# A decoder of mixed layers on one core: routed experts in two groups of blocks instead of one

## The chip, the cores and the metric

The kernel runs on one core of a Trainium2 chip. The metric is the device time of one execution in microseconds; the median over runs counts. Its engines are PE (matrix products; its weight loads are listed as PEld), DVE (vector), ACT (activations), POOL (the general engine, which also issues the scatters), and SP, which issues the plain DMAs. Each works through its own queue in order, and they wait for each other by semaphores.

## What is computed

Twelve layers follow each other on 2048 tokens of width 128 (32 sequences of 64), each with a residual and a layer norm: `x = layernorm(x + layer(x))`. Three of them matter here. Before the change's place comes a cross attention with 16 heads of width 8 (`l1x`), then a layer of experts (`l1f`), then a causal self attention of the same heads (`l2a`). The expert layer sends each token through one of eight two-layer networks, the one whose logit is largest:

```python
logits = xf @ Wr.T + br
expert_idx = jnp.argmax(logits, axis=-1)
h = jax.nn.relu(jnp.einsum('td,efd->etf', xf, W1) + b1[:, None, :])   # 128 -> 512
y = jnp.einsum('etf,edf->etd', h, W2) + b2[:, None, :]                 # 512 -> 128
out = y[expert_idx, jnp.arange(xf.shape[0])]
```

## The kernel before

Tokens lie in four blocks of 512 (`NBLK`), each of four tiles of 128 tokens. Work is written as steps: `sp.at(step, place, f)` puts a piece of work at a step and a place in it, and `Steps.run` (L269) calls the pieces in that order. PE's instructions keep exactly this order. DVE's and ACT's keep it only in the stretches in `sp.fixed` (from four steps before the end of the experts on); elsewhere a scheduler orders them, and it orders POOL's and SP's everywhere.

The attention (`attn8`, L675) goes through 16 units, four to a block: scores with mask (`s`), maximum and difference on DVE (`mx`, `p`), the exponential on ACT, transposes (`ptps`, copied by ACT to `pT`), values (`o`), normalising on DVE (`rec`, `a`), a transpose (`aT`) and the output product (`y`), then sum and layer norm. The layer norm's `rstd` (L436) is two operations on POOL. The last block is handled in halves.

The expert layer is `sorted_experts` (L1441). While the attention runs, `routed` (L1381) does, for pieces of tiles: logits (`rps`, L343), the comparison and the first best expert on DVE, a running count per expert (`before`, `tally` L1332), ranks by two products (`inc`, `rank` L1345), the row of each token (`slot`), and one indirect DMA per token tile from POOL (L1364) that scatters the tokens' rows, each with its token number, into a DRAM buffer `sorted_x`, in which every expert has room for all 2048 tokens.

When all tokens are counted, `tables` (L1460) takes one product for the totals (`cnt`) and some fifteen small DVE operations to a table: for each of `NTL = 16 + 7 = 23` tiles of 128 sorted rows, its expert and its first row. The engines then read the table's numbers into registers (`values_load`, L1497) and use them as addresses: SP for the load of each tile's rows (`xsorted`, L1379), ACT for a copy of the expert's first weights, 512 columns (L1508), DVE for a copy of its second weights and biases, 644 columns (L1510), both out of the big buffer `wbig` where all eight experts lie. A tile (`tile_`, L1546) is then a transpose (`xsT`, L1514) of the tile two ahead, the first product (`hps`, four matmuls), a relu with bias in four parts (`hs`, two on ACT at L1530 and two on DVE at L1528, in turn), and for the tile before it the second product (`yps`), the sum with the bias on DVE (`ysorted`, L1541) and a scatter of the rows into `token_y` by token number (L1364), issued by POOL. All 23 tiles stand at one step after the attention.

On the way back, `rows_back` loads a block's rows from `token_y` after all scatters (`z`), DVE adds the residual, the layer norm follows, `turn_x` transposes (`xTps`, copied to `xT`), and the next attention's keys, queries and values (`proj`, `k`, `kx`, `q`, `vps`) of block 0 start. Block 0's norm is done by DVE and ACT in halves; the others' come at later steps. Between the last tile and block 0's transposes stand the keys and values of three blocks of a later cross attention (`early`, L705), which only need the context; their results lie in `wbig` over weights no longer needed.

Of the kernel before, what the change touches and what calls it, by code (L numbers as in the profile page):

```python
# [30 lines left out]
NTL = NTT + NEXP - 1  # L31
XR = D + 4
SORTED = NEXP * NT + NEXP * P - P
# [10 lines left out]
def _constants():  # L44
# [12 lines left out]
    c["base1"] = np.broadcast_to((e * f(NT) - f(1)) / f(P), (P, 8))  # L57
    c["base2"] = np.broadcast_to((e * f(CAP) - f(1)) / f(P), (P, 8))
    c["less1"] = np.broadcast_to(e * f(NT) - f(P), (P, 8))
# [222 lines left out]
class Decoder:  # L282
# [66 lines left out]
    def setup(self):  # L349
# [42 lines left out]
        self.sorted_x = self.tc.dram_tile([SORTED, XR], F32, name="sorted_x")  # L392
        self.chosen_x = self.tc.dram_tile([NEXP * CAP, XR], F32, name="chosen_x")
        self.token_y = [self.tc.dram_tile([NT, D], F32, name=f"token_y{i}") for i in range(2)]
# [15 lines left out]
    def clear(self, sp, first):  # L410

        self.cleared = []
        zero = {}

        def start():
            z = zero[0] = self.q2([P, 3, XR], "zero")
            self.nc.gpsimd.memset(z, 0.0)
            self.nc.gpsimd.memset(z.bitcast(I32)[:, :, D:], 1 << 16)

        def part(dst, o, n, m, d):  # L420
            v = dst[o : o + P * n * m, :].rearrange("(p n m) d -> p n m d", n=n, m=m)
            i = self.nc.sync.dma_start(v, bc(zero[0][:, 0:m, 0:d], 1, n))
            self.cleared.append(i.ins)

        sp.at(first, 7, start)
        parts = [(self.sorted_x, i * P * 15, 5, 3, XR) for i in range(9)]
        parts += [(self.chosen_x, 0, 5, 1, XR), (self.token_y[1], 0, 16, 1, D)]
        for i, p in enumerate(parts):
            sp.at(first + 1 + 2 * i, 7, lambda p=p: part(*p))
# [245 lines left out]
    def attn8(self, sp, base, name, src=None, rope=None, scale=1.0, row=None, mask=(None, None), has_out=True, split=False, number=False, turned=None, ahead=None, held=False):  # L675
# [136 lines left out]
        sp.at(base - 4, 2.4 if held else 3, start)  # L812
# [5 lines left out]
        for blk in range(NBLK):  # L818
            for i in range(3):
                n = base + 4 * blk - 4  # L820
                at = (n + 1 + (i + 1) // 2, 4 + i % 2 / 2) if held and blk else (n + i, 4)
                sp.at(*at, lambda blk=blk, i=i: prepare(blk, i))
            sp.at(base + 4 * blk + (1 if split and not has_out else 2), 5.5, lambda blk=blk: resid(blk))
            if halved(blk):
                sp.at(*((base + 16, 6.5) if turned is None else (base + 16, 5.8)), lambda blk=blk: turn(blk, (0, 2)))
                sp.at(*((base + 17, 6.5) if turned is None else (base + 17, 2.1)), lambda blk=blk: turn(blk, (2, 2)))
                sp.at(*((base + 16, 6.4) if turned is None else (base + 16, 5.3)), lambda: normal_rest(0))
                sp.at(*((base + 17, 6.4) if turned is None else (base + 17, 2)), lambda: normal_rest(1))
            else:
                at = (base + 4 * blk + 8, 6)  # L830
                if split and blk == NBLK - 2:
                    at = (base + 16, 2.1 if has_out else 4.1)
                sp.at(*at, lambda blk=blk: turn(blk, (0, TPB)))
# [498 lines left out]
    def tally(self, st, t0, n, base):  # L1332

        before = st["before", t0] = self.sb([P, TPB + 1, 8], "before", 3)
        last = st.get("sum", base)
        self.nc.gpsimd.tensor_copy(before[:, 0, :], last)
        for t in range(n):  # L1340
            self.tt(before[:, t + 1, :], last, st["oh"][:, t0 + t, :], ALU.add)
            last = before[:, t + 1, :]
        st["sum"] = last
# [37 lines left out]
    def routed(self, sp, st, ready, wr, br, base, rows, dst, bound, gated):  # L1381


        def logits(t0, i):
# [18 lines left out]
        def chosen(t0, n):  # L1403
            self.first_of(st.pop(("lg", t0))[:, 0:n, :], st["oh"][:, t0 : t0 + n, :])
            self.tally(st, t0, n, self.c[base])
# [5 lines left out]
        def scatter(t0, t):  # L1411
            blk, i = divmod(t0 + t, TPB)
            self.scatter(
                dst, self.xfull[blk][:, i, :], st["at", t0][:, t : t + 1], st["done"], self.cleared, bound
# [10 lines left out]
        ]  # L1425
        for t0, m, logit, compared, first, second, ranked, scattered in pieces:
# [14 lines left out]
    def sorted_experts(self, sp, name, ready, fetched, tiles, back):  # L1441
# [5 lines left out]
        k = dict(done=[], y=[])  # L1447
# [12 lines left out]
        def tables():  # L1460

            ps = self.ps8("G", "cnt")
            self.mm(ps[:, 0:8], self.ones, k["sum"])
# [14 lines left out]
            table = k["table"] = self.once([P, 2, NTL], "tiles", I32)  # L1478
            jump = self.once([P, 8], "jump")
            nc.vector.tensor_scalar(jump, size, -1.0, float(NT), ALU.mult, ALU.add)  # L1480
# [8 lines left out]
            for j in range(NTL):  # L1489
                if j % 3 == 0:  # L1490
                    xg[j // 3] = self.q2([P, 3, XR], "xsorted")
                row = number(1, j, SORTED - P, mybir.EngineType.SP)
                self.load_after(xg[j // 3][:, j % 3, :], self.sorted_x[bass.ds(row, P), :], k["done"])
            for j in range(AHEAD):
                weights(j)

        def number(i, j, most, engine):  # L1497
            return nc.values_load(
                k["table"][0:1, i, j : j + 1], engines=[engine], min_val=0, max_val=most,
# [3 lines left out]
        def weights(j):  # L1503
            if j < NTL:
                w1, w2 = wts[j] = self.q2([P, 4 * P], "w1"), self.q4([P, EROW - 4 * P], "w2")
                most = (NEXP - 1) * EROW
                at = number(0, j, most, mybir.EngineType.Activation)
                nc.scalar.copy(w1, self.big[:, bass.ds(at, 4 * P)])  # L1508
                at = number(0, j, most, mybir.EngineType.DVE) + 4 * P
                nc.vector.tensor_copy(w2, self.big[:, bass.ds(at, EROW - 4 * P)])  # L1510

        def turn(j):
            ps = self.ps8("G", "xsT")
            nc.tensor.transpose(ps[:, 0:P], xg[j // 3][:, j % 3, 0:D], self.ident)  # L1514
            xT = self.sb([P, P], "xsT", 3)
            nc.scalar.copy(xT, ps[:, 0:P])
            st[j] = xT

        def hidden(j):
            ps = self.ps8("G", "hps").rearrange("p (c n) -> p c n", n=P)  # L1520
            w1, w2 = wts[j]
            for c in range(4):
                self.mm(ps[:, c, :], w1[:, c * P : (c + 1) * P], st[j])
            h = self.q2([P, 4, P], "hs")
            for c in range(4):
                b1 = w2[:, 4 * P + c : 4 * P + c + 1]
# [4 lines left out]
            st[j] = h  # L1531

        def second(j):
            h, (_, w2) = st.pop(j), wts.pop(j)
            ps = self.ps8("G", "yps")
            for c in range(4):
                self.mm(ps[:, 0:D], h[:, c, :], w2[:, c * P : (c + 1) * P], c == 0, c == 3)
            if j % 4 == 0:
                ys[j // 4] = self.q2([P, 4, D], "ysorted")
            y = ys[j // 4][:, j % 4, :]  # L1540
            self.summed = nc.vector.tensor_tensor(out=y, in0=ps[:, 0:D], in1=w2[:, 4 * P + 4 :], op=ALU.add).ins  # L1541
            at = xg[j // 3].bitcast(U32)[:, j % 3, D : D + 1]
            self.scatter(self.token_y[0], y, at, k["y"], [], NT - 1)
            weights(j + AHEAD)

        def tile_(j):  # L1546
            if j == 0:
                turn(0)
                turn(1)
            if j + 2 < NTL:  # L1550
                turn(j + 2)
            hidden(j)
            if j:
                second(j - 1)
            if j == NTL - 1:
                second(j)

        def rows_back(b):
            z[b] = self.q2([P, TPB, D], "z")
            self.load_after(z[b], self.token_rows(0, b), k["y"] + [[], [self.turned_at], [self.wide], [self.wide]][b])  # L1560

        def added(b):
            self.tt(z[b], z[b], self.xt[b], ALU.add)
            if b:
                k["moments", b] = self.moments(b, z[b])
            else:
                self.norm(b, z.pop(b), "both")
# [11 lines left out]
        sp.at(ready + 10, 0, tables)  # L1579
        for j, at in enumerate(tiles):  # L1580
            sp.at(*at, lambda j=j: tile_(j))
        sp.at(tiles[-1][0], tiles[-1][1] + 0.05, lambda: rows_back(0))
        for b in range(NBLK):
            if b:
                sp.at(*back[b][0], lambda b=b: rows_back(b))
            sp.at(*back[b][1], lambda b=b: added(b))
            if b:
                sp.at(back[b][1][0] + 1, 0.5, lambda b=b: negated(b))
                sp.at(back[b][1][0] + 1, 6.4, lambda b=b: ended(b))
            sp.at(*back[b][2], lambda b=b: self.turn_x(b))  # L1590


    def capacity_experts(self, sp, name, ready, fetched, tiles, back):
        nc = self.nc
        k = dict(done=[], y=[])
# [19 lines left out]
        def loads():  # L1615
            self.ready_for(AF.Gelu_apprx_tanh, k["gate"][:, NTT - 1 : NTT])
            v = self.chosen_x.rearrange("(e p) d -> p e d", p=CAP)
            for g in range(0, NEXP, 3):
                n = min(3, NEXP - g)
                xg[g // 3] = self.q2([P, 3, XR], "chosen")  # L1620
                self.load_after(xg[g // 3][0:CAP, 0:n, :], v[:, g : g + n, :], k["done"])
# [16 lines left out]
        def second(e):  # L1638
# [11 lines left out]
            self.scatter(self.token_y[1], y, at, k["y"], self.cleared, NT - 1)  # L1650
# [13 lines left out]
        def rows_back(b):  # L1664
            z[b] = self.q2([P, TPB, D], "z")
            self.load_after(z[b], self.token_rows(1, b), k["y"] + [[], [self.turned_at], [self.wide], [self.wide]][b])
# [15 lines left out]
        def ended(b):  # L1682
# [3 lines left out]
            sp, k, ready, self.w[name]["wr"], self.rows["l2f_br"], "base2", rows, self.chosen_x, NS - 1, True  # L1686
# [182 lines left out]
def decoder_kernel(ctx: ExitStack, tc: tile.TileContext, ins, at, out):  # L1869
# [21 lines left out]
    tiles = [(n, 0.1 + 0.1 * j) for j in range(NTL)]  # L1891
    n = n + 4
    back = [
        (None, (n - 4, 3.5), (n - 4, 3.6)), ((n - 4, 3.7), (n - 1, 5), (n + 1, 2.5)),
        ((n + 1, 4.5), (n + 3, 6), (n + 5, 3.5)), ((n + 5, 4.5), (n + 7, 6), (n + 9, 3.5)),
    ]
    k.sorted_experts(sp, "l1f", ready, (n - 16, 7), tiles, back)
    sp.fixed.append((n - 7, n + 33))
    k.attn8(sp, n, "l2a", scale=s8, row=rows["l2a_bo"], mask=("heads", "alibi"), held=True)
    ahead = (n - 4, 2.6, 3)  # L1900
# [45 lines left out]
```

## Time and profile before

| what | value |
| --- | --- |
| runs | 1405.1, 1413.34, 1413.83 us, median 1413.34 |
| profiled execution | 1401.48 us, its span 1399.1 us |
| busy: PE, PE loads | 1191.9 us (85%), 863.5 us (62%) |
| busy: DVE, ACT, POOL | 932.1 us (67%), 686.0 us (49%), 741.9 us (53%) |
| granted TensorE clock, mean | 0.927 |
| last score group of `l1x` ends | 857.5 us |
| first tile's transpose, last scatter of results issued | 891.5 us, 941.2 us |
| first and fourth score group of `l2a` start | 959.73 us, 978.90 us |

The profile page lists the busy time of each engine, the span in 40 slices, the chain of work that ended last and the costliest groups. A group reads: line, engine, operation, written tile <- read tiles, shapes, count, busy time, and what ended the idle time before it. A timeline reads: start, length, engine, line, operation, tiles, shapes, count, and in brackets the engine's idle time just before and what ended it. PE's length for a product counts hardware passes: one product of float32 is two passes. A row of windows lists for each engine its busy time in that stretch and its number of instructions, then the granted TensorE clock, the share of the DMA engines and GB/s.

### The profile page before, as it was taken

To read this page: it belongs to the slowest core of one execution; us is meant where nothing else is said; L and a number is where in the kernel's file an instruction comes from. 1 tells how busy PE (TensorE), PEld (TensorE's weight loads), DVE (VectorE), ACT (ScalarE), POOL (GpSimd) and SP (SyncE) were. 2 spreads that over 40 slices of the span, in tenths; PEclk is the share of its full clock that TensorE was granted. 3 is DMA by queue.
4 is the path that set the end of the run, shared out by engine and by line. 5 is a ranking of instruction groups with operands and counts; after the bars stand their busy time and mean duration, and the time that the engine had idled before them with its cause. 6 is when DMAs were issued, how large, how long until landed. Compare 5 with 4: busy or idle time off the path is not lost.

```text
span 1399.1 us, 37035 instructions
## 1 busy us (share of the span) xinstructions
PE 1191.9 (85%) x16009; PEld 863.5 (62%) x16009; DVE 932.1 (67%) x1856; ACT 686.0 (49%) x1172; POOL 741.9 (53%) x618
## 2 busy tenths in 40 slices
PE   7998877988888878998898998597999948889991
PEld 4776545655655555666667777594778737567771
DVE  5765767777776776756656566464668853766797
ACT  2453445555455545454455554364556524344552
POOL 3533688777776764444544245353346543336553
PEclk9999899999999989999999999697999968889995
DMA  6010010053010000010001100221001101000001
GB/s 242 2 18 11 1 47 1 1 181 122 1 56 1 1 1 2 2 69 2 2 2 36 36 2 25 69 75 34 9 2 42 44 10 28 9 9 3 2 2 30
DMA packets 33715, 43.16 MB, mean 31 GB/s; under 512 B 5947, under 2 KB 27122, under 8 KB 33169
## 3 DMA queue, kind: packets, MB, share of 16 engines
q1 hardware_dynamic: 31536, 38.20, 8.6%
q8 instruction: 126, 2.06, 0.6%
q0 software_dynamic: 2016, 2.60, 0.6%
q14 instruction: 37, 0.30, 0.1%
HBM read 26.63 MB, written 15.56 MB: 30 GB/s over the span
## 4 chain that ended last, share of the span: by engine, by line
PE 50%; DVE 21%; POOL 13%; ACT 9%; issue 5%; DMA 2%; POOLq 0%; SPq 0%; DVEq 0%; ACTq 0%
PE s L343 10%; PE o L343 9%; DVE turn L346 6%; PE proj L343 5%; POOL turn L346 5%; PE qkps L343 5%; PE ptps L669 4%; PE y L343 4%; PE ropeT L971 3%; ACT pT L671 2%; DVE p L346 2%; DVE rn L1131 2%; POOL token_y L1364 2%; POOL rstd L346 2%; POOL rn L346 2%
## 5 line engine op out<-in xcount | busy, mean ns | idle before, releaser
L346 POOL TENSOR_TENSOR turn<-turn,turn 128x1024 f32<-128x1024 f32 x64 | 150.6, 2361 | 94.3 <-DVE turn L346 93.7
L656 DVE TENSOR_REDUCE mx<-s 128x16 f32<-128x1024 f32 x96 | 117.3, 1222 | 109.0 <-PE s L343 108.9
L346 DVE TENSOR_TENSOR p<-s,mx 128x1024 f32<-128x1024 f32 (+1 forms) x144 | 159.0, 1104 | 5.8
L671 ACT COPY pT<-ptps 128x512 f32<-128x512 f32 x192 | 103.3, 588 | 73.7 <-PE ptps L669 72.8
L726 ACT ACTIVATE p<-p 128x1024 f32<-128x1024 f32 x96 | 101.4, 1056 | 52.6 <-DVE p L346 52.4
L343 PE MATMUL s<-kx,q 32*64 32x128 f32 x3072 | 109.1, 280 | 5.2 <-DVE sparts L1727 3.4
L346 DVE TENSOR_TENSOR turn<-qkps,w_const 128x512 f32<-128x512 f32 (+1 forms) x96 | 75.9, 861 | 55.6 <-PE qkps L343 55.6
L343 PEld LDWEIGHTS s<-kx,q 32*64 32x64 f32 x3072 | 85.5, 135 | 36.8 <-issue 28.9
L669 PE MATMUL ptps<-w_const,p 128*128 128x128 f32 x768 | 105.7, 282 | 0.6 <-ACT p L726 0.5
L440 POOL TENSOR_SCALAR rstd<-bnmv 128x4 f32<-128x4 f32 (+1 forms) x60 | 16.1, 269 | 164.8 <-DVE bnmv L489 145.7
L971 PE MATMUL ropeT<-w_const,turn 128*128 128x128 f32 x512 | 70.9, 285 | 29.7 <-ACT oT L1029 13.8
L594 POOL TENSOR_TENSOR kx<-k,w_const 128x1024 f32<-128x1024 f32 x31 | 60.2, 1960 | 67.1 <-ACT k L603 30.9
L346 POOL TENSOR_TENSOR rn<-rn,nhalf 128x16 f32<-128x16 f32 x32 | 93.8, 2930 | 2.7
L669 PEld LDWEIGHTS ptps<-w_const,p 128*128 128x128 f32 x768 | 87.0, 145 | 9.8 <-issue 8.2
L343 PEld LDWEIGHTS o<-v,pT 128*64 128x64 f32 x2176 | 71.9, 139 | 31.3 <-ACT pT L671 15.2
L971 PEld LDWEIGHTS ropeT<-w_const,turn 128*128 128x128 f32 x512 | 59.4, 146 | 41.3 <-ACT oT L1029 13.1
L343 PE MATMUL o<-v,pT 128*64 128x18 f32 x2176 | 80.0, 214 | 5.1 <-ACT pT L671 4.0
L346 DVE TENSOR_TENSOR turn<-qkps,xtab 128x512 f32<-128x512 f32 (+1 forms) x96 | 82.1, 859 | 0.0
L343 PE MATMUL o<-pT,v 64*64 64x64 f32 x2048 | 71.7, 223 | 10.2 <-ACT pT L1013 10.2
L509 POOL TENSOR_SCALAR x<-z,bnmv,rstd 128x128 f32<-128x128 f32 x98 | 78.3, 811 | 2.6
L1131 DVE TENSOR_REDUCE rn<-sq 128x16 f32<-128x1024 f32 x32 | 39.0, 1218 | 58.8 <-ACT sq L1127 58.8
L343 PEld LDWEIGHTS o<-pT,v 64*64 64x64 f32 x2048 | 64.9, 137 | 17.3 <-ACT pT L1013 12.6
(345 smaller groups left out, 2785.7 us busy)
## 6 DMA issues: line engine op xcount, KB each, us to landing
sorted_x<-zero SPq DMA_DIRECT2D x9, 990.0 KB, 13.2
wbig<-in_l1f_w_dram SPq DMA_DIRECT2D x4, 1156.0 KB, 6.6
wbig<-in_l2f_w_dram SPq DMA_DIRECT2D x16, 256.0 KB, 3.2
wbig<-in_l0f_dram SPq DMA_DIRECT2D x2, 1561.0 KB
z<-token_y SPq DMA_DIRECT2D x8, 256.0 KB, 2.7
wbig<-in_l1a_dram SPq DMA_DIRECT2D x1, 1856.0 KB, 7.7
xsorted<-sorted_x SPq DMA_DIRECT2D x23, 66.0 KB, 1.8
xT<-in_xT_dram SPq DMA_DIRECT2D x4, 256.0 KB, 6.8
```

Source lines behind the costliest of these rows:

```text
L343: self.nc.tensor.matmul(out, lhsT=lhsT, rhs=rhs, start=start, stop=stop)
L346: (eng or self.nc.vector).tensor_tensor(out=out, in0=a, in1=b, op=op)
L440: nc.gpsimd.tensor_scalar(r[:, :n], var, EPS, None, ALU.add)
L509: eng.tensor_scalar(x[:, t0 + t, :], z[:, t0 + t, :], mv[:, t, 0:1], r[:, t : t + 1], ALU.subtract, ALU.mult)
L594: self.wide = eng.tensor_tensor(out=kx, in0=bc(kT, 1, 2), in1=bc(head[:, 2 * i : 2 * i + 2], 2, TB), op=ALU.mult).ins
L656: nc.vector.tensor_reduce(mx, s3, AX.X, ALU.max)
L669: self.nc.tensor.transpose(ps[:, j, :], flat[:, c : c + P], self.ident)
L671: self.nc.scalar.copy(o, ps)
L726: nc.scalar.activation(prs[n], prs[n], AF.Exp)
L971: self.nc.tensor.transpose(pt[:, j * P : (j + 1) * P], f[:, j * P : (j + 1) * P], self.ident)
L1131: nc.vector.tensor_reduce(rn, sq, AX.X, ALU.add)
L1364: i = self.nc.gpsimd.indirect_dma_start(dst, bass.IndirectOffsetOnAxis(at, 0), src, None, bounds_check=bound, oob_is_err=False).ins
```

## The change

The expert layer is done in two groups: blocks 0 and 1, then blocks 2 and 3 (`NGRP = 2`, `NG = 1024` tokens, `NTL = 8 + 7 = 15` tiles each, 30 in all). Each group has its own `sorted_x`, `token_y`, counts, table and lists of scatters. The routing's pieces come at earlier places. The first group's table is built at the last step but one of the attention, eight of its tiles stand among the attention's last pieces of work and the routing of the last block, and the other seven right after the second group's table. The second group's tiles stand where all 23 stood; among them stand block 0's load, sum, norm and transposes and the next attention's first keys, queries and values. Block 1's rows are loaded right behind the second group's tiles; blocks 2 and 3 wait for the second group's scatters as they waited for all before.

The weights are used in place: only the first ones are copied, 256 columns by ACT and 256 by DVE; PE reads the second weights, ACT and DVE the biases out of `wbig` at register addresses. PE, too, now reads the table, once per tile, and has an address computation before each of a tile's four second products.

`early` for the later cross attention moves from the way back to just behind the first score group of `l2a`. In the last block of `l1x` the second half's norm and transposes move ahead within their step.

```diff
-NTL = NTT + NEXP - 1
+NGRP = 2
+NG = NT // NGRP
+NTL = NG // P + NEXP - 1
...
-        self.sorted_x = self.tc.dram_tile([SORTED, XR], F32, name="sorted_x")
+        self.sorted_x = [self.tc.dram_tile([SORTED, XR], F32, name=f"sorted_x{g}") for g in range(NGRP)]
...
-                sp.at(*((base + 17, 6.5) if turned is None else (base + 17, 2.1)), lambda blk=blk: turn(blk, (2, 2)))
+                sp.at(*((base + 17, 4.06 if number and name == "l1x" else 6.5) if turned is None else (base + 17, 2.1)), lambda blk=blk: turn(blk, (2, 2)))
...
+        if len(dst) > 1:
+            for i, b in enumerate((n, n + 4)):
+                sent = [(b + 3, 2.5), (b + 3, 2.6), (b + 3, 5.5), (b + 3, 5.6)]
+                pieces[i] = (4 * i, 4, [(b + 1, 1.5), (b + 1, 4.5)], (b + 1, 5.6), (b + 1, 5.61), (b + 2, 5.6), (b + 3, 1.5), sent)
+            pieces[3:] = [
+                (12, 2, [(n + 9, 1.5)], (n + 9, 1.6), (n + 9, 4), (n + 9, 4.1), (n + 9, 4.2), [(n + 9, 4.21)] * 2),
+                (14, 2, [(n + 9, 4.5)], (n + 9, 4.51), (n + 9, 4.6), (n + 9, 4.65), (n + 9, 4.7), [(n + 9, 4.8)] * 2),
+            ]
...
-                w1, w2 = wts[j] = self.q2([P, 4 * P], "w1"), self.q4([P, EROW - 4 * P], "w2")
...
-                nc.scalar.copy(w1, self.big[:, bass.ds(at, 4 * P)])
-                at = number(0, j, most, mybir.EngineType.DVE) + 4 * P
-                nc.vector.tensor_copy(w2, self.big[:, bass.ds(at, EROW - 4 * P)])
+                w1 = self.q2([P, 4 * P], "w1")
+                at = [
+                    number(g, 0, j, most, e)
+                    for e in (mybir.EngineType.Activation, mybir.EngineType.DVE, mybir.EngineType.PE)
+                ]
+                nc.scalar.copy(w1[:, 0 : 2 * P], of(at[0], 0, 2 * P))
+                nc.vector.tensor_copy(w1[:, 2 * P :], of(at[1], 2 * P, 2 * P))
+                wts[g, j] = [w1] + at
...
+        def of(at, o, n):
+            return self.big[:, bass.ds(at + o, n)]
...
-                self.mm(ps[:, 0:D], h[:, c, :], w2[:, c * P : (c + 1) * P], c == 0, c == 3)
+                self.mm(ps[:, 0:D], h[:, c, :], of(pe, (4 + c) * P, P), c == 0, c == 3)
...
-    tiles = [(n, 0.1 + 0.1 * j) for j in range(NTL)]
+    s = ready + 8
+    amid = [(s, 6.15), (s, 6.55), (s + 1, 0.6), (s + 1, 1.2), (s + 1, 1.7), (s + 1, 4.07), (s + 1, 4.3), (s + 1, 4.55)]
+    tiles = [
+        ((s - 1, 5.8), amid + [(s + 1, 6 + 0.1 * j) for j in range(NTL - len(amid))]),
+        ((s + 1, 5), [(n, 0.1 + 0.1 * j) for j in range(NTL)]),
+    ]
     n = n + 4
     back = [
-        (None, (n - 4, 3.5), (n - 4, 3.6)), ((n - 4, 3.7), (n - 1, 5), (n + 1, 2.5)),
...
+        ((s + 1, 7), (n - 4, 0.55), ((n - 4, 0.75), (n - 4, 0.76)), (n - 4, 0.95)),
+        ((n - 4, 1.65), (n - 1, 5), ((n, 0.5), (n, 6.4)), (n + 1, 2.5)),
...
+    sooner = [(n - 4, 0.75), (n - 4, 1.05), (n - 4, 1.15), (n - 4, 1.25)]
...
-    ahead = (n - 4, 2.6, 3)
+    ahead = (n, 4, 3)
```

## The prediction

> **What bounds the kernel now.** I read the windows by stage first, then the chain of waits, then the timeline of each engine between 857 and 980 us, and last the order in which the changed kernel issues its instructions. The order of all engines is the same as before up to the last units of the cross attention (near 845 us) and again from the fourth score group of the next attention on (near 979 us), so only this stretch can change. Its marks: the last score group of the cross attention ends at 857.5, and the first of the next attention starts at 959.73: 102.2 us.
>
> The windows show PE as the bound on both sides and in the tiles, with poor stretches between. Columns: busy of PE, PE loads, DVE, ACT, POOL, then the granted clock.
>
> ```profile
> 860.00:880.00 20.00, 10.79 (x127) 9.88 (x126) 8.48 (x50) 4.71 (x9) 12.26 (x18) 0.76 0.16 48
> 880.00:900.00 20.00, 10.19 (x54) 9.13 (x54) 8.75 (x41) 5.37 (x15) 4.08 (x5) 0.55 0.20 51
> 900.00:920.00 20.00, 20.00 (x179) 19.90 (x179) 13.87 (x42) 14.68 (x42) 11.04 (x11) 1.00 0.26 68
> 940.00:960.00 20.00, 12.60 (x146) 7.36 (x144) 7.05 (x20) 8.78 (x15) 8.69 (x11) 0.74 0.33 101
> ```
>
> The chain of waits (start, length, what) names the poor stretches: routing, then scatter and load of the sorted rows, then 23 tiles, then the way back.
>
> ```profile
> 886.99 2.28 DMA sorted_x<-x,slot
> 889.53 1.84 DMA xsorted<-sorted_x
> ...
> 941.22 0.98 POOL token_y L1364
> ...
> 944.85 2.87 DMA z<-token_y
> ```
>
> It follows the tiles along POOL, but the PE timeline shows PE without a pause there: a tile is one transpose and two groups of matmuls, and transposes start 1.90 us apart. 23 tiles are 43.7 us.
>
> ```profile
> 902.38 0.27 PE L1514 MATMUL xsT<-w_const,xsorted 128*128 128x128 f32 x1
> 902.49 1.06 PE L343 MATMUL hps<-xsT,w 128*128 128x128 f32 x8
> 903.39 1.06 PE L343 MATMUL yps<-w,hs 128*128 128x128 f32 x8
> 904.28 0.27 PE L1514 MATMUL xsT<-w_const,xsorted 128*128 128x128 f32 x1
> ```
>
> **The change, part by part.** Every position below is in microseconds of the profiled execution. It took 1401.48, span 1399.1, which is 11.9 under the median of the runs (1413.34); I work out a difference on it and apply that to the median.
>
> *Tiles.* Two groups of 15 instead of 23: 30 x 1.90 = 57.0 us of PE, 13.3 more. What is won must come from the poor stretches, which the first group should fill.
>
> *First table.* The first group's table is now built while the attention still runs, and PE itself reads it (three register reads right after the count product). PE's queue is in order, so the attention's last transposes, products and logits stand behind that wait. The count product is done at about 860.9 (the values of the last unit but one end at 860.16, plus small products). DVE must first finish the last scores, a reciprocal and two products: 861.3. The table took 3.54 (884.89 to 888.43); its four widest operations (1.44 together) shrink by 8/23, so 3.0. From its end to the first reader on ACT (889.23) were 0.80; each further read with its address costs SP 20.35 / 23 - 0.45 = 0.43.
>
> ```profile
> 0.73 0.39 SPq L320 DMA_DIRECT2D w_const<-in_const_dram  x1
> 1.18 0.42 SPq L320 DMA_DIRECT2D w_l0a<-in_l0a_dram  x1
> ...
> 889.53 20.35 SPq L1379 DMA_DIRECT2D xsorted<-sorted_x  x23
> ```
>
> So PE goes on at 861.3 + 3.0 + 0.8 + 0.9 = 866.0, where it went on at 861.13: 4.9 lost. The rest of the attention took 6.9 (861.13 to 868.04); ACT's queue now has three weight copies before four pT copies, 3 x 0.26 = 0.8. The first tile starts at 873.7; before, its transpose started at 891.50.
>
> *POOL's detour.* The last half block still needs its mean and deviation, whose rstd stands in POOL's queue behind four scatters of sorted rows and two of results. The first of them can go at about 878.1: DVE does three copies, a sum, statistics, two scalings and the slots before, about 4.4 us of rows of 0.19 to 0.48 plus POOL's 0.24 + 0.72. Scatters that wait for nothing stand 1.28 apart (939.94, 941.22). 878.1 + 6 x 1.28 + 1.1 = 886.9; DVE waits for it with two scalings, and the relus of tile 3 are queued behind them, about 1.4: tile 3's second product starts at 888.3 instead of about 884.5.
>
> *To the second table.* Four tiles (7.6) and six small products (1.6): the second count is done at 897.5. Own, slots, table, reads on PE: 0.4 + 3.0 + 0.8 + 0.9 = 5.1, so 902.6; again nothing of PE can pass.
>
> *Tiles 8 to 14.* 7 x 1.90 = 13.3, plus 1.2 (relus behind the copies at the start) and 1.5 (the last tile has nothing to cover its relus): 918.6. SP's loads (0.885 each) and the row scatters of the second group are done by about 915, so its first tiles wait for none. On SP the load of block 0's rows now stands ahead of the next expert layer's weights, which must wait until the last tile has read the big buffer; those are wanted only near 1155 (second expert layer, first product), so their delay of some 15 us costs nothing.
>
> *Second group.* 28.5, plus what is woven in for the next attention (transposes 0.45, two projections 2.1, values 1.08, bias 0.2: 3.8), plus filling and draining 2.3 and 0.5 for the statistics: 35.1, so 953.7. The way back of block 0 (944.85 to 954.45 before) is covered by these tiles: its scatters end near 920, its load takes 2.9, and its sum is wanted only after tile 4, near 928. If that cover were gone it would cost its old 9.6.
>
> *Register reads on PE.* Each tile adds one read and four address computations to PE's queue. On ACT, copies behind their own reads start 0.52 apart and plain ones 0.48: 0.04 where work is queued. After a wait ACT shows 0.43 from relu to copy instead of 0.26:
>
> ```profile
> 900.58 0.37 ACT L1530 ACTIVATE hs<-hps,w 128x128 f32<-128x128 f32 x1 [0.42 <-DVE hs L1528]
> 901.01 0.62 ACT L1508 COPY w<-wbig 128x512 f32 x1
> ```
>
> PE has work queued, so I take 0.05 per tile, 1.5 in all. Bounds: 0, since PE's 34 passes fill the 1.90, and 0.43 + 3 x 0.2 = 1.0 per tile, 30 us. [...] ACT's 0.17 after a wait says that a queue does not hide all.
>
> *Clock.* After an idle of 4.01 us PE ran at about half speed for some 5 us (32 score matmuls in 1.13; 0.69 elsewhere):
>
> ```profile
> 505.90 1.13 PE L343 MATMUL s<-qk,qk 64*64 64x64 f32 x32 [4.01 <-ACT qk L972]
> 506.96 1.11 PE L1011 MATMUL ptps<-w_const,p 128*128 128x128 f32 x4
> 507.86 1.92 PE L343 MATMUL y<-wbig,oT 128*128 128x128 f32 x8
> ```
>
> Both table waits are that long: 2 x 2.5, of which POOL's detour hides more than half: 2.0. Bounds 0 and 5. [...]
>
> *Weights in place.* ACT's copy goes from 512 to 256 columns, DVE's from 644 to 256; the second product reads the big buffer. In the tiles ACT's round (copy 0.52, copy 0.19, relu, DVE, relu, 0.43) was 1.9 too, so this only keeps ACT from being the bound: nothing. Without it the round would stay at 1.9 plus address computations.
>
> *Moved: the early keys and values.* They stood in the way back (PE 940.07 to 945.76, hidden) and now follow the first score group; ACT's nine copies (5.9) now stand before block 1's scaling, and POOL's memsets (2.8) after the last scatter. Fourth minus first score group was 978.90 - 959.73 = 19.2, in which PE ran at half clock (projections 2.08 for 1.13). Now: ACT reaches block 1's scaling 9.6 after the first score group, the third group starts at 13.8 instead of 9.9, but then goes at full clock, 5.9 instead of 9.2: 19.7, 0.5 more.
>
> *Sum.* 953.7 + 1.5 + 2.0 = 957.2 against 959.73: -2.5; +0.5 makes -2.0. That is 1411 on the median. A measurement of this kernel can tell about 1%, 14 us, from no change.
>
> **Rivals.**
> A, slower: PE's register work is not hidden. Per tile PE would need over 0.12 for any loss, and over 0.58 for a loss past 1%. For it: four of the five steps stand between matmuls of 0.22, and ACT's 0.17. Against: 0.04 in a run of copies. At 0.6: +16.5 - 2 = +14.5, 1428.
> B, faster: the waits cost nothing, because other work of PE lies in them or the attention's end has slack: 4.9 + 5.1 + 3.8 + 2.0 = 15.8 off, -17.8, 1396. For it: the old stage idles twice for 6.6 us. Against: PE's order has nothing between count and reads.
> C, POOL becomes the bound: from 878.1 on 38 scatters x 1.28 = 48.6 and about 6 of others end near 933, before 953. At the old spacing of 1.9 they end near 956: no change either, about 1414.
> D, the tiles do not fill anything, and the second group pays the old way back: +9.6, 1421. Against: block 0's rows are needed 8 us after they land.
>
> **How the numbers follow.** Forecast 0.45, A 0.22, B 0.20, C 0.05, D 0.08. Of A, 0.18 lies past 1%; of B, 0.17 (it needs nearly all its terms). Forecast, C, D and the rests are within 1%: 0.65. The forecast's own range is its bounds: clock -2 to +3, reads -1.5 to +6, waits each 2 either way: 1403 to 1421. The whole range reaches B at 1396 and A at 1428, leaving out about 0.2 beyond.
>
> **What would show it.** Right: tiles' transposes 1.9 to 2.0 apart in both groups; two idles of PE of 4 to 5 us ended by the table; an idle near the fourth tile ended by POOL's rstd; first score group of the next attention near 957. Wrong: tiles over 2.2 apart with PE waiting on issue (A); count and reads without a PE idle (B); the second group's tiles waiting for scatters (C), or block 0's sum waiting for its load (D).

## The result, and the profile after

The changed kernel took 1423.67 us (median of four runs, 1420.23 to 1429.32) against 1409.22 for the kernel before in the same comparison: a ratio of 1.0105, 95% interval 1.0059 to 1.015. A second comparison, on another chip, gave 1.0101 (1.006 to 1.0141). So it is slower by 1%, about 14 us, where 2 us less were forecast.

The windows of the first changed profile (1429.32 us, span 1427.5), the same stretches as shown of before; columns as there:

```profile
860.00:880.00 20.00, 11.23 (x124) 9.95 (x117) 9.82 (x46) 6.43 (x12) 8.48 (x12) 0.69 0.19 48
880.00:900.00 20.00, 15.74 (x136) 14.30 (x135) 10.13 (x43) 7.66 (x25) 8.48 (x11) 0.88 0.22 60
900.00:920.00 20.00, 13.05 (x89) 12.31 (x87) 9.25 (x48) 5.63 (x17) 8.85 (x9) 0.83 0.14 40
940.00:960.00 20.00, 17.40 (x133) 14.96 (x131) 11.88 (x44) 12.18 (x36) 10.44 (x11) 1.00 0.10 29
```

The poor stretch of 880 to 900 (PE 10.2 before) is better filled, but 900 to 920, which held tiles without a pause, now has 7 us of idle PE. In this profile the chain of waits between 860 and 900 names other links than before: no DMA any more, but PE behind a register read ("issue"), DVE's sum, and scatters ahead of `rstd` on POOL. (The chain of the second profile still passes a scatter and a load of sorted rows.)

```profile
866.86 1.21 issue
...
877.65 0.43 DVE z L348
878.12 3.61 PE o L345 x64
...
892.78 1.00 POOL token_y L1372
...
894.89 0.80 POOL rstd L348
```

This first profile also holds stretches in which PE's results seem to have been announced late. DVE starts here on a product that ended, by PE's own row, at 890.30; 0.86 us of the time between are a wait of DVE. (The ends of PE's rows are modelled, so the row may instead end too early.)

```profile
889.69 0.61 PE L345 MATMUL y<-w_l1x,aT 128*128 128x128 f32 x4
```
```profile
893.33 0.42 DVE L348 TENSOR_TENSOR z<-y,resid 128x256 f32<-128x256 f32 x1 [0.86 <-remote]
```

Waits of this kind also stand near 841 to 846 and 1129 to 1135, outside the changed stretch (DVE's maximum starts at 841.18, 0.65 us after its score group ended by PE's row, and at 1129.05, 2.05 us after). In the second profile of the same kernel (1407.11 us) none of these is there, so I compare the forecast with that one. To compare profiles I shift each so that the last query projection of the cross attention falls on 829.9, where it was before (it stands at 820.1 in the second changed profile). Marks after the shift:

| mark | forecast | changed kernel | reads later (e5) | reads later, early work spread (e11) |
| --- | --- | --- | --- | --- |
| first count on PE | 860.9 | 860.6 | 860.6 | 860.6 |
| PE goes on | 866.0 | 865.8 | 861.6 | 861.6 |
| first tile's transpose | 873.7 | 879.4 | 873.1 | 871.9 |
| second count on PE | 897.5 | 904.5 | 897.9 | 897.9 |
| PE goes on | 902.6 | 909.2 | no wait | no wait |
| second group starts | 918.6 | 927.7 | 914.7 | 914.7 |
| first score group of `l2a` (before: 959.7) | 957.2 | 965.2 | 952.2 | 952.2 |
| fourth (before: 978.9) | 976.9 | 990.3 | 977.1 | 971.6 |

At the fourth score group the changed kernel is 13.4 us later than forecast and 11.4 later than before. From there to the end this profile takes another 4.6 us more than the one before, where nothing was forecast to change. That part differs between profiles (4.2 more with the reads later, 1.5 more in e9, the run with PE's reads early), and its cause stays open. The lines behind the second column, PE's timeline of the second profile:

```profile
850.77 0.39 PE L345 MATMUL cnt<-before,ones 128*128 128x8 f32 x2
855.97 0.66 PE L770 MATMUL aT<-w_const,a 128*128 128x128 f32 x2 [4.81 <-issue]
856.42 1.92 PE L674 MATMUL ptps<-w_const,p 128*128 128x128 f32 x8
...
866.04 3.61 PE L345 MATMUL o<-v,pT 128*64 128x18 f32 x64 [3.33 <-DVE z L348]
869.59 0.90 PE L1541 MATMUL xsT<-w_const,xsorted 128*128 128x128 f32 x3
...
899.36 0.45 PE L1541 MATMUL xsT<-w_const,xsorted 128*128 128x128 f32 x1 [4.27 <-issue]
```

The two waits for a table are there, as long as forecast (4.81 and 4.27 idle). What was not forecast are the 3.33 behind DVE, and the durations: `ptps` 1.92 for 1.04 before, `o` 3.61 for 2.05, both at half clock (0.50 granted). `o` in the profile before:

```profile
865.99 2.05 PE L343 MATMUL o<-v,pT 128*64 128x18 f32 x64
```

### The profile page after: what moved, and what is told of

The parts are those of the page before. It is cut to its first block, busy times and chain, and to the rows that moved or that the text cites. A ratio compares the mean times of both kernels' runs of the same rounds, so it can differ in the third digit from the quotient of the medians.

```text
span 1427.5 us, 37737 instructions
## 1 busy us (share of the span) xinstructions
PE 1230.0 (86%) x16130; PEld 895.4 (63%) x16130; DVE 938.4 (66%) x1898; ACT 692.3 (48%) x1202; POOL 747.1 (52%) x625
## 4 chain that ended last, share of the span: by engine, by line
PE 53%; DVE 20%; POOL 11%; ACT 9%; issue 4%; DMA 1%; DVEq 0%; POOLq 0%; SPq 0%; ACTq 0%
PE s L345 11%; PE o L345 9%; DVE turn L348 5%; PE qkps L345 5%; PE ptps L674 5%; PE proj L345 5%; POOL turn L348 4%; PE y L345 3%; PE ropeT L979 3%; ACT pT L676 2%; DVE p L348 2%; DVE rn L1139 2%; PE hps L345 2%; POOL rstd L348 2%; POOL rn L348 2%
## 5 line engine op out<-in xcount | busy, mean ns | idle before, releaser
L674 PE MATMUL ptps<-w_const,p 128*128 128x128 f32 x768 | 111.0, 291 | 0.9 <-ACT p L732 0.5
L345 PEld LDWEIGHTS o<-v,pT 128*64 128x64 f32 x2176 | 76.1, 145 | 36.5 <-ACT pT L676 15.7
L674 PEld LDWEIGHTS ptps<-w_const,p 128*128 128x128 f32 x768 | 91.7, 150 | 9.8 <-issue 7.9
L345 PE MATMUL o<-v,pT 128*64 128x18 f32 x2176 | 84.4, 218 | 8.9 <-ACT pT L676 4.0
L345 PE MATMUL o<-pT,v 64*64 64x64 f32 x2048 | 70.4, 220 | 10.2 <-ACT pT L1021 10.2
L345 PE MATMUL qkps<-wbig,hT 128*128 128x512 f32 x128 | 70.7, 681 | 6.6 <-POOL hT L1115 5.0
```

Of the source, the lines that this page charges most:

```text
L345: self.nc.tensor.matmul(out, lhsT=lhsT, rhs=rhs, start=start, stop=stop)
L674: self.nc.tensor.transpose(ps[:, j, :], flat[:, c : c + P], self.ident)
```

## The experiments

All ratios are to the kernel before, from comparisons of its own on one chip, with 95% intervals.

**The changed kernel again.**

> The changed kernel unaltered, for a second profile and a closer interval. In the first profile PE's results were late in three stretches (841 to 846, 888 to 895, 1129 to 1135 us), each with half clock after it. If these are chance, they are gone or elsewhere here, the way from the cross attention's last score group to the next attention's first one is some 103 to 110 us (109.7 in the first profile, 102.2 before), and the second routed layer starts no later than in the kernel before, apart from the shift. If they belong to the change, they come at the same places. The ratio to before: 1.008 to 1.013 either way.

Measured: 1.0101 (1.006 to 1.0141), 1413.27 against 1399.59. The late results are gone from this profile, the ratio stayed, and the fourth score group is still 11.4 us late, so they are not the cause; the two waits and the slow first score groups of `l2a` came again at the same places.

**Weights copied again, in two groups.** PE has no register reads in this kernel.

```diff
-                nc.scalar.copy(w1[:, 0 : 2 * P], of(at[0], 0, 2 * P))
-                nc.vector.tensor_copy(w1[:, 2 * P :], of(at[1], 2 * P, 2 * P))
...
+                nc.scalar.copy(w1, of(at, 0, 4 * P))
...
+                nc.vector.tensor_copy(w2, of(at, 4 * P, EROW - 4 * P))
```

> The two groups stay, but the weights are copied as before the change (512 columns on ACT, 644 on DVE) and PE has no register reads. If PE's register reads and addresses are exposed (rival A of the prediction), the tiles get shorter and the ratio falls to 1.003 or less. If they lie behind matmuls (the forecast: 0.05 a tile), tiles in the second group stay 1.9 us apart where nothing else stands between them, and the ratio stays within 1.008 to 1.016, the upper end if ACT becomes the bound of the tiles.

Measured: 1.0025 (0.9995 to 1.0055). The ratio falls, as rival A wanted, but the tiles do not get shorter: they were 1.9 apart already. What is gone are the waits behind both counts. In the profile others stand in their place: `o` waits 4.21 for DVE's sum, and one tile behind the second table 2.27 and 1.65 for its relus.

**Weights in place, one group.** The kernel before, with this part of the change alone.

> The kernel before the change, with only the weights read in place (PE reads the table and computes four addresses per tile; one group of 23 tiles). If register work on PE is hidden: transposes 1.90 us apart as before and a ratio of 0.998 to 1.002. If it is exposed: 23 tiles x 0.3 or more, 7 us, ratio 1.005 or more.

Measured: 0.9976 (0.9944 to 1.0009). Three tiles of it, with the table read and four address computations of PE in each:

```profile
904.89 0.27 PE L1520 MATMUL xsT<-w_const,xsorted 128*128 128x128 f32 x1
905.00 1.06 PE L343 MATMUL hps<-xsT,w 128*128 128x128 f32 x8
...
906.86 0.27 PE L1520 MATMUL xsT<-w_const,xsorted 128*128 128x128 f32 x1
...
908.75 0.27 PE L1520 MATMUL xsT<-w_const,xsorted 128*128 128x128 f32 x1
```

The transposes are 1.97 and 1.89 us apart, 1.90 before. Register work on PE is hidden in a run of tiles; rival A's mechanism falls. What is left for a register read to cost is the wait for its value (4.81 us behind the first count in the second profile of the changed kernel).

**Reads issued later.** The first three weight reads of each group move from the table to the place where they are needed.

```diff
-            for j in range(AHEAD):
-                weights(g, j)
...
+            for j in range(AHEAD):
+                sp.at(*reads[g], lambda g=g, j=j: weights(g, j))
...
+    reads = [(s, 6.14), (s + 1, 6.55)]
```

> The changed kernel, in which the first three weight reads of each group (ACT, DVE and PE) are issued later: for the first group just ahead of its first tile, for the second behind the first group's last tile. So no work of PE stands behind a register read that waits for a table. Theory: the two waits (4.9 and 4.3 us in the second profile of the changed kernel) go, and with them most of the half clock behind them and the three weight copies that stood ahead of a sum on DVE: 8 to 12 us, ratio 0.998 to 1.005, two idles of PE fewer. Rival (other waits, such as the scatters on POOL and the rows' loads, end last anyway): at most 3 us gained, ratio 1.008 or more.

Measured: 1.0025 (0.9996 to 1.0054), 0.0076 or some 11 us less than the change. PE's timeline:

```profile
852.32 0.39 PE L345 MATMUL cnt<-before,ones 128*128 128x8 f32 x2
853.32 0.44 PE L770 MATMUL aT<-w_const,a 128*128 128x128 f32 x2 [0.60 <-DVE slot L1422]
853.59 1.59 PE L674 MATMUL ptps<-w_const,p 128*128 128x128 f32 x8
854.97 1.06 PE L539 MATMUL xTps<-w_const,x 128*128 128x128 f32 x4
...
861.01 3.61 PE L345 MATMUL o<-v,pT 128*64 128x18 f32 x64 [1.17 <-DVE z L348]
```

The wait of 4.81 is gone, and the one behind DVE's sum shrank from 3.33 to 1.17. Half clock is still there (0.50 granted): `ptps` takes 1.59 and `o` 3.61, though PE sat idle only 0.60 and 1.17 before them.

**Only the first group's reads later.** The place of the second group's reads stays behind its table, `reads = [(s, 6.14), (s + 1, 5)]`.

> As the run before, but only the first group's weight reads are issued later; the second group's stay behind its table. Theory: about half of what that run gains, 4 to 7 us, ratio 1.003 to 1.007, with one idle of PE of 4.3 us left, ended by the second table. Rival (the first table's wait is covered by rows and scatters that come no earlier): ratio 1.008 or more.

Measured: 1.0016 (0.999 to 1.0041), as much as with both. The expected 1.003 to 1.007 is missed. By the medians the first group's reads are the loss and the second wait costs nothing that can be told. A single profile says otherwise for the second (first score group of `l2a` at 958.5 with it, 952.2 without it, after the shift); the two intervals leave room for that, so the second wait's price stays open.

**PE's reads early, the others late.** PE's three reads stay behind the count; ACT's and DVE's reads and copies move to the places of the run with both groups' reads later.

```diff
             for j in range(AHEAD):
-                weights(g, j)
+                k["pe", g, j] = number(g, 0, j, (NEXP - 1) * EROW, mybir.EngineType.PE)
```

> As the run with the weight reads issued later, but PE's first three reads of each group stay right behind the count, as in the change; only ACT's and DVE's reads and copies come later. This takes the sum on DVE out from behind the three copies and leaves PE's two waits. Theory (PE's waits are the loss): ratio 1.007 to 1.010, close to the change. Rival (DVE's queue is the loss): ratio 1.005 or less.

Measured: 1.0107 (1.0078 to 1.0136), the loss of the change in full. So it is PE's wait, by the medians. The one profile does not show it as well: it is the fastest of the six executions (1404.45, median 1413.39), and its fourth score group stands at 984.3 after the shift, between 977.1 with all reads later and 990.3 in the changed kernel. The queue on DVE was a real step in the changed kernel, as its timeline (second profile) shows, three copies ahead of the sum that `o` waits for,

```profile
864.35 0.29 DVE L1533 COPY w<-wbig 128x256 f32 x1 [0.86 <-DMA xsorted<-sorted_x]
864.86 0.29 DVE L1533 COPY w<-wbig 128x256 f32 x1 [0.22 <-issue]
865.36 0.29 DVE L1533 COPY w<-wbig 128x256 f32 x1 [0.21 <-issue]
865.57 0.42 DVE L348 TENSOR_TENSOR z<-y,resid 128x256 f32<-128x256 f32 x1
```

but taking it away alone changed no median. (In the first of these lines the bracket names a DMA that landed at that moment. In e5 the same pause, 0.84, is put down to an ACT copy, and the chain of the first profile has DVE's register read in it.)

**No tiles among the attention.** `amid` is empty; all 15 tiles of the first group follow the second table.

> The changed kernel, in which all 15 tiles of the first group stand behind the second table, none among the last units of the attention. Theory: the eight woven tiles do fill idle time of PE (some 8 x 1.9 less what they add in waits): without them 6 to 12 us slower than the changed kernel, ratio 1.014 to 1.019. Rival (woven in, they gain nothing, since they run at half clock and behind scatters): ratio 1.007 to 1.012.

Measured: 1.0126 (1.0091 to 1.016). That lies between the two expectations and cannot be told from the change: beside PE's wait, no gain from the weaving shows here.

**Early keys and values back in their old place.**

```diff
-    ahead = (n, 4, 3)
+    ahead = (n - 4, 2.6, 3)
```

> Only the early keys and values go back to where they stood before the change (after the last tile, ahead of the next attention's first score group). Theory: in the new place their 5.7 us of PE delay block 1's rows through ACT's copies and leave two idles of PE, with half clock behind them; first to fourth score group took 25.3 us in the changed profile and 19.2 before. Back in the old place the first score group comes 5.7 later and the fourth 19 to 20 after it: about nothing to 6 us gained, ratio 1.006 to 1.010. Rival (the move costs nothing, the loss is all ahead of it): the ratio stays at 1.0105 or gets worse by up to 0.003.

Measured: 1.0122 (1.0081 to 1.0163): the theory is not borne out, and the measured ratio is where the rival put it. First to fourth score group took 19.6 us, as expected (25.1 in the changed kernel's second profile), but the first came 7.15 later, counted from the first count on PE. With the way back covered by tiles, this work is on the path in either place, by this profile.

**Early keys and values moved in the kernel before.** The reverse edit, `ahead = (n, 4, 3)`, in the kernel before the change.

> The kernel before the change, with only the early keys and values moved behind the next attention's first score group. In the kernel before they fill the way back, where PE waits. Theory: the prediction's +0.5 us for this step was wrong; 5.7 us of PE come onto the path and half clock stays: 4 to 7 us, ratio 1.003 to 1.005, first to fourth score group 24 to 26 us after each other instead of 19.2. Rival (the prediction's step): ratio within 0.999 to 1.002.

Measured: 1.0018 (0.9989 to 1.0046). First to fourth score group took 24.8 us, for 19.2 before, so the profile bears the theory out. The time does not: it moved by less than the theory had it, not clear of zero, and to where the rival put it.

**Early keys and values spread.** One block behind the first score group, one behind the second, one behind block 1's transposes.

```diff
-                    sp.at(step, place + 0.1 * i, lambda blk=blk, i=i: early(blk, i))
+                    at = (step, place) if m == 4 else ((step, place), (step + 1, 1), (step + 1, 3))[blk]
+                    sp.at(at[0], at[1] + 0.1 * i, lambda blk=blk, i=i: early(blk, i))
```

> The changed kernel, in which the three blocks of early keys and values stand apart: one behind the first score group as in the change, one behind the second, one behind block 1's transposes, into PE's two idles there (0.8 and 1.2 us), so that block 1's scaling on ACT waits for three copies and not for nine. Theory: first to fourth score group falls from 25.1 to 19 to 22 us, with less half clock: 3 to 6 us gained, ratio 1.006 to 1.008. Rival (the 5.7 us of PE are on the path wherever they stand, and the clock halves anyway): at most 1.5 us gained, ratio 1.009 or more.

Measured: 1.0081 (1.0054 to 1.0107). First to fourth score group fell to 19.4 us. The gain in time, 0.002 or 3 us, is at the lower end of the theory and not clear of zero.

**Both: reads later and early work spread.**

> Weight reads issued later in both groups, and the early keys and values spread as in the run before. Theory: the gains add: 1.0025 less 0.002 to 0.004, so 0.998 to 1.0005, which a measurement can't tell from the kernel before the change. Rival (the kernel is held by something else behind this place): 1.002 or more.

Measured: 0.9959 (0.9932 to 0.9986), 1391.71 against 1398.65: faster than the kernel before, by more than the theory had it. Its first score groups of `l2a` come first here, then those of the changed kernel (second profile):

```profile
952.72 1.13 PE L345 MATMUL s<-alibi,ident 128*128 128x512 bf16 x4
...
956.95 1.14 PE L345 MATMUL s<-alibi,ident 128*128 128x512 bf16 x4
...
964.88 1.12 PE L345 MATMUL proj<-xT,w_l2a 128*128 128x512 f32 x2 [1.10 <-ACT xT L542]
965.85 1.13 PE L345 MATMUL s<-alibi,ident 128*128 128x512 bf16 x4
...
972.14 1.14 PE L345 MATMUL s<-alibi,ident 128*128 128x512 bf16 x4
```
```profile
955.42 1.13 PE L345 MATMUL s<-alibi,ident 128*128 128x512 bf16 x4
...
963.23 1.14 PE L345 MATMUL s<-alibi,ident 128*128 128x512 bf16 x4
...
966.17 1.49 PE L539 MATMUL xTps<-w_const,x 128*128 128x128 f32 x4 [0.77 <-ACT x L533]
968.88 2.07 PE L345 MATMUL proj<-xT,w_l2a 128*128 128x512 f32 x2 [1.23 <-ACT xT L542]
970.75 1.82 PE L345 MATMUL s<-alibi,ident 128*128 128x512 bf16 x4
...
980.52 1.14 PE L345 MATMUL s<-alibi,ident 128*128 128x512 bf16 x4
```

The projections take 1.12 in the first and 2.07 in the second. The same work, with one idle of 1.10 in place of 0.77 and 1.23 and without half clock, takes 19.4 in place of 25.1. Against the run with the reads later alone (1.0025) the intervals do not touch, so here the spreading shows in the time too.

## Why the prediction was wrong

**What failed: the clock.** Two steps went wrong: the clock term of the sum, 2.0 with bounds 0 and 5, and in the moved work that the third group "then goes at full clock". The windows of the second profile cut at the recorded stretches of half clock (columns as above):

```profile
852.40:859.20 6.80, 3.23 (x16) 3.26 (x16) 2.05 (x13) 0.37 (x1) 3.79 (x4) 0.50 0.12 41
862.60:876.30 13.70, 10.38 (x97) 9.89 (x96) 5.60 (x26) 3.09 (x10) 2.87 (x5) 0.50 0.26 65
896.70:903.60 6.90, 4.24 (x20) 4.27 (x21) 1.64 (x9) 0.34 (x2) 1.58 (x2) 0.51 0.19 53
968.40:978.70 10.30, 9.82 (x79) 6.38 (x80) 2.45 (x2) 3.60 (x6) 4.97 (x3) 0.50 0.09 25
```

PE was busy for 27.67 us of them. If PE was the bound all through, half of that, 13.8, is what half clock cost: 8.9 ahead of the next attention and 4.9 in its first score groups. That is an estimate. I had 2.0 in all, so it accounts for 11.8 of the 13.4 us. In the profile before PE was busy at half clock for 26.0 us of this stretch:

```profile
870.50:897.80 27.30, 10.84 (x46) 9.71 (x47) 10.30 (x55) 3.98 (x11) 10.38 (x15) 0.50 0.22 60
949.00:959.30 10.30, 6.14 (x30) 3.00 (x32) 3.31 (x11) 2.84 (x5) 3.25 (x3) 0.50 0.09 26
966.10:976.30 10.20, 9.06 (x68) 5.35 (x69) 3.26 (x3) 4.43 (x7) 4.97 (x3) 0.50 0.06 17
```

I took the poor clock for a companion of the long idles and let it go with them; by these two profiles it stayed, and now there was work in it. The runs with fewer waits say the same. With all reads later (e5) PE is still busy at half clock for 22.2 us, and the ratio is 1.0025; with the early work spread as well (e11) for 12.7, and the kernel is faster than before:

```profile
853.90:857.30 3.40, 3.40 (x18) 3.29 (x17) 2.10 (x13) 1.55 (x4) 2.79 (x3) 0.50 0.13 42
860.70:870.90 10.20, 9.74 (x92) 9.29 (x93) 4.40 (x20) 3.14 (x11) 2.32 (x5) 0.50 0.28 69
956.30:966.50 10.20, 9.09 (x77) 5.77 (x78) 2.62 (x3) 3.84 (x6) 4.98 (x3) 0.50 0.09 26
```
```profile
866.70:876.90 10.20, 9.19 (x91) 8.38 (x90) 5.31 (x27) 3.87 (x11) 1.94 (x4) 0.50 0.25 68
887.20:890.70 3.50, 3.50 (x20) 3.36 (x18) 2.03 (x11) 1.08 (x3) 1.26 (x3) 0.51 0.08 23
```

The profile that I started from was lucky, too. The rest of the attention (6.9 us) ran at full clock in it. The kernel with weights in place (e4) and the one with only the early work moved (e7) have the old order there, and in both profiles half clock begins 8 us earlier (after the shift), `o` takes 3.61 for 2.05, and the first of the stretches holds 22 us of busy PE for 10.84:

```profile
858.10:895.60 37.50, 22.02 (x145) 19.82 (x143) 13.97 (x83) 6.57 (x16) 14.37 (x20) 0.50 0.15 45
```
```profile
853.90:891.50 37.60, 22.08 (x145) 19.89 (x144) 14.83 (x83) 6.88 (x16) 14.42 (x19) 0.50 0.16 46
```

So half clock at the attention's end is not the change's doing, and how much of it there is differs between executions. In all these two have some 39 and 37 us of it, more than the changed kernel's 27.7: what the change does to half clock can't be told from single profiles.

In the second profile the first stretch of half clock, 852.40 to 859.20, begins inside the first wait, an idle of 4.81 us. With the reads later (e5) the ones from 853.90 and 860.70 stand at idles of only 0.60 and 1.17, so in these runs half clock also comes without a long idle.

**The other 1.6 us** are roughly the net of: DVE's sum behind the three copies, which the forecast did not have (3.33 - 1.17 = 2.2); the second group, 37.6 for 35.1, with 1.5 of it where a relu on DVE stands behind block 0's sum (2.5); the rest of the attention, the tiles beside these and the moved work, 0.8 more; and what I had put too high: register reads 1.5, POOL's detour 1.9 (I had 3.8, and PE idled 1.9 for it), the second table 0.5.

**The range** was added up wrongly at its upper end: 1411 with the bounds as written (+3, +6 and twice +2) is 1424, not 1421. Measured against the kernel before of the same comparison, +14.4 lies beyond either.

**What held.** First count, both waits, the way back covered by tiles, tiles at 1.90 us, register reads hidden: the marks up to 865.8 are within 0.3. The first score group of `l2a` came at 965.2 instead of 957.2, with the sum. The changed kernel without PE's waits (e5) passes the first tile and the second count within 0.6 of the forecast made with them, which is luck: two errors of opposite sign.

**The cause of the loss.** Kernels in which PE reads the first table right behind the count: 1.0101, 1.0122, 1.0126, 1.0107, 1.0081 (e1, e2, e8, e9, e10). Kernels with two groups in which it does not: 1.0025, 1.0025, 1.0016, 0.9959 (e3, e5, e6, e11). That is shown, by the medians; single profiles do not part the two sets as clearly (fourth score group at 984.3 in e9, 984.2 in e3 and 983.6 in e6, after the shift). The wait was in my sum with 4.9 and a part of the clock term; taken away it is worth 0.0085 (e6), about 12 us with an uncertainty of some 7, more than the 6.6 by which the second count moves in e5. It did not take the half clock with it: e6's profile has some 27 us of it, e10's only some 18 at a ratio of 1.0081. Half clock accounts, by the estimate, for the distance to the forecast, not for which of these kernels is slower. As I read the profiles, the sign came out wrong because what I set against the wait, the half clock that should go, did not go; no run shows that by itself.

**The rivals.** A's time came true without its mechanism: register work is hidden (tiles 1.97 and 1.89 us apart in e4, 1.90 before), the register's wait is not (4.81 and 4.27 us in the second profile). B names the right lever: without the waits, though with the detour still there (PE idles 1.96), the kernel comes to 1.0025 and not to -17.8 us. By its profile the fourth score group is 16 us later than B would have it, and half of the 22.2 us at half clock is 11 of these. C and D did not happen; no tile waited for scatters, and block 0's sum did not wait for its load.

**What stays open.** Why half clock comes at the end of the attention without a long idle, before the change as after it, and when it stays away; what the second wait costs; and whether two groups beat one group with weights in place (0.9959 and 0.9976, with overlapping intervals).

## What to carry to other kernels

In these runs a register read on PE was a wait for the value, at the place where it was written: 4.81 and 4.27 us of idle PE in the second profile of the changed kernel, gone with the reads later (e5). Put it just ahead of its first use, not behind the table, and ask what stands behind it in that queue. When a change fills a poor stretch, do not also book the clock as won: 27.67 us of PE's work ran at 0.50 in the second profile. Price the filled work at half clock as one end of the range. The moved work was hidden while it lay in a gap, the way back before the change. With that gap filled by tiles it was, by e2's profile, on the path in either place (1.0101 behind the first score group, 1.0122 back in the old place), and spreading it over small idles is what won it back, once the reads were later (1.0025 in e5, 0.9959 in e11).

## What the runs showed that I had not expected

Half clock begins without a long idle (0.60 and 1.17 us in e5) and lasts over 10 us of busy PE (9.82 us busy of 10.30 in the second profile). Its stretches in the rows above last 3.4 to 37.6 us, each within 0.2 of a multiple of 3.4 (6.8, 10.2, 13.7, 27.3, 37.5). In one profile PE's results seem to have been announced up to 3.0 us late (890.30 to 893.33) in places that a second run of the same kernel passed on time. Single executions of one kernel spread by over 1% (1386.67 to 1402.06 in e11), so one profile's marks do not replace the medians.
